# Leaving one token of each batch out of a projection, and one column out of each score tile

## The chip, the cores and the metric

One core of a Trainium2 chip. The metric is the device time of one execution of the whole program, in microseconds (us). A run is compared only with runs of the kernel before on the same chip.

## The reference, cut to what matters

128 batches of 64 tokens with 768 features go through two layers of attention on a graph. Everything is FP32.

```python
h = relu(layernorm(x))
for l in range(2):
    m_left  = einsum('bsh,oh->bso', h, W_left[l])
    m_right = einsum('bsh,oh->bso', h, W_right[l])
    u_left  = einsum('bih,bjh->bij', h, m_left)  / sqrt(768)
    u_right = einsum('bih,bjh->bij', h, m_right) / sqrt(768)
    # on and above the diagonal the left score counts, below it the right one
    u = u_left * triu(adj, k=0) + u_right * swapaxes(triu(adj, k=1), 1, 2)
    e = exp(u) * adj
    attention = e / (sum(e, axis=2) + 1e-10)
    h = relu(layer_norm(attention @ (h @ W_lin[l].T + b_lin[l])))
out = x + h
```

A right score is used only for j < i. So `m_right` of the last token of a batch (j = 63) is used by no row at all. That is what the change removes.

## The kernel before

Each layer has two passes over 16 blocks of 512 tokens (8 batches). Pass one makes `m_left` and `m_right` of a block ("project") and then, one block late, the scores and the softmax. Pass two makes the linear part, the attention times it, and the normalization. A projection is done as 15 products of sums of weight blocks and sums of token blocks, 256 tokens wide, whose results VectorE and ScalarE read out of the bank and add into `M`. The two halves k = 0 (left) and k = 1 (right) lie side by side in `M`, 64 columns each.

```python
# project(u, k): 15 products, each with 2 x 2 matmuls of 128 x 128 by 128 x 256
p = bank[at].rearrange("p (g t) -> p g t", g=2)
for g in range(2):
    for c in range(K2):
        nc.tensor.matmul(p[:, g], w[ORDER[i][0]][:, c, g * P:(g + 1) * P], b()[t][:, c, :],
                         start=(new and g == c == 0), stop=(c == K2 - 1), skip_group_check=True)
...
read(p.rearrange("p g (b s) -> p g b s", s=S),
     lambda o: M[u][:, o // 2 * K2:(o // 2 + 1) * K2, o % 2 * 4:o % 2 * 4 + 4, k, :], i, seen)
...
# scores(u): rows 0-31 of a batch need left 0-63 and right 0-30,
# rows 32-63 need left 32-63 and right 0-62
for e in (0, 32):
    nc.tensor.matmul(p[h * S + e:h * S + e + 32, q, e:e + 96],
                     ht[:, c, b * S + e:b * S + e + 32], mb[:, e:e + 96],
                     start=(c == 0), stop=(c == C - 1))
```

Of the kernel before, what the change touches and what calls it, by code (L numbers as in the profile page):

```python
# [13 lines left out]
ALU = mybir.AluOpType  # L14
# [3 lines left out]
def kernel(  # L18
# [24 lines left out]
    nc = tc.nc  # L43
    B, S, H = x.shape
    L = w_lin.shape[0]
    P = 128
    C = H // P
    HH = H // 2
    K2 = 2
# [5 lines left out]
    NB = B * S // T  # L55
# [13 lines left out]
    NBB = T // S  # L69
# [17 lines left out]
    def run(slot):  # L87
        if slot in plan:
            for f in plan.pop(slot):
                f()  # L90
        elif idle:
            f = idle.popleft()
            if f is not None:
                f()
# [14 lines left out]
    ORDER = ((8, "X", "ta", "+2"), (5, "Z", "u1", "-0+2"), (0, "X", "u2", "+3"), (1, "Y", "u3", "-3"),  # L109
             (12, "X", "B3", "-5"), (6, "V", "B0", "-2"), (2, "X", "td", "-4"), (4, "Y", "tb", "+1"),  # L110
             (10, "X", "B4", "+0-2"), (7, "V", "B1", "+3"), (3, "X", "u0", "+1-3"), (11, "Y", "te", "+0"),
             (13, "V", "tc", "-1"), (9, "Z", "tg", "+4"), (14, "V", "tf", "+5"))
# [31 lines left out]
    def added(eng, o, sign, a, b):  # L144
        (eng.tensor_add if sign == "+" else eng.tensor_sub)(o, a, b)  # L145
# [13 lines left out]
    def tokens_of(key):  # L159
        ht = HT[key]  # L160
        r = {f"B{2 * j + t}": ht[:, j * K2:(j + 1) * K2, t * TH:(t + 1) * TH] for j in range(3) for t in range(2)}
        r.update(TS.get(key, {}))
        return r

    def sums_t(key, eng=nc.gpsimd):
        ts = TS[key] = {}

        def one(o, s, m, n):
            t = big.tile([P, K2, TH], F32, name="ts", bufs=13)
            b = tokens_of(key)  # L170
            added(eng, t, s, b[m], b[n])
            ts[o] = t

        return [lambda x=x: one(*x) for x in T_SUMS]
# [8 lines left out]
    def read(p, to, i, seen):  # L183

        what = ORDER[i][3]
        for n in range(0, len(what), 2):
            sign, o = what[n], int(what[n + 1])
            if o not in seen:
                seen.add(o)
                nc.scalar.activation(to(o), p, AF.Copy, scale=1.0 if sign == "+" else -1.0)  # L190
            else:
                added(nc.vector, to(o), sign, to(o), p)
# [20 lines left out]
    for h in range(PAIR):  # L213
        r = slice(h * S, (h + 1) * S)
# [153 lines left out]
    def pass_one(l, aside):  # L368
        with tc.tile_pool(name=f"one{l}", bufs=2, reuse_waits="tile") as sp:
            ADJ, CHAIN, M = {}, {}, {}  # L370
# [25 lines left out]
            def project(u, k, just):  # L396


                b, w = lambda: tokens_of((1, l, u)), W[l, "lr"[k]]
                bank, seen = {}, set()  # L400
                for i, (at, t, _) in ((i, (o[1], o[2], o[3])) for i, o in enumerate(ORDER)):
                    new = i in FIRST
                    if new:
                        bank[at] = ps_st.tile([P, 2 * TH], F32, name=at)
                    p = bank[at].rearrange("p (g t) -> p g t", g=2)
                    for g in range(2):
                        for c in range(K2):
                            nc.tensor.matmul(p[:, g], w[ORDER[i][0]][:, c, g * P:(g + 1) * P], b()[t][:, c, :],  # L408
                                             start=(new and g == c == 0), stop=(c == K2 - 1), skip_group_check=True)
                        if g == 0:  # L410
                            run(30 * k + 2 * i)
                    if i == 0 and k == 0:
                        if u:
                            scores(u - 1)
                        M[u] = sp.tile([P, C, NBB, 2, S], F32, name="m", bufs=1)
                    read(p.rearrange("p g (b s) -> p g b s", s=S),
                         lambda o: M[u][:, o // 2 * K2:(o // 2 + 1) * K2, o % 2 * 4:o % 2 * 4 + 4, k, :], i, seen)
                    for f in just.get(i, ()):
                        f()
                    run(30 * k + 2 * i + 1)  # L420

            def scores(u):



                ht, m, adj = HT[1, l, u], M[u], ADJ[u]
                p = ps_aux.tile([P, 2, T], F32, name="aux")[:, 0].rearrange("p (q m) -> p q m", q=Q)
                for q in range(Q):
                    for c in range(C):
                        for h in range(PAIR):  # L430
                            b = q * PAIR + h
                            mb = m[:, c, b].rearrange("p k j -> p (k j)")
                            for e in (0, 32):
                                nc.tensor.matmul(p[h * S + e:h * S + e + 32, q, e:e + 96],  # L434
                                                 ht[:, c, b * S + e:b * S + e + 32], mb[:, e:e + 96],
                                                 start=(c == 0), stop=(c == C - 1))

                def chain():

                    wm = sp.tile([P, Q, 2, S], F32, name="wm", bufs=1)  # L440
                    for k in range(2):
                        nc.gpsimd.tensor_tensor(wm[:, :, k], adj[:, :, 1 - k],
                                                tri[:, k].unsqueeze(1).to_broadcast([P, Q, S]), op=ALU.mult)
                    yield
                    flat = wm.rearrange("p q k j -> p (q k j)")
                    for i in range(0, P, 32):
                        r = wm.rearrange("p q k j -> p q (k j)")[i:i + 32, :, i % S:i % S + 96]
                        nc.vector.tensor_tensor(r, p[i:i + 32, :, i % S:i % S + 96], r, op=ALU.mult)  # L448
                        if i % S:
                            yield  # L450
                    v = adj[:, :, 0, :]
                    nc.vector.tensor_add(v, wm[:, :, 0], wm[:, :, 1])
                    yield
                    nc.scalar.activation(v, v, AF.Exp, scale=ISTEMPER)
                    yield
                    nc.vector.tensor_mul(v, v, adj[:, :, 1, :])
                    s = stat.tile([P, Q], F32, name="s", bufs=2)
                    nc.vector.reduce_sum(s, v, axis=mybir.AxisListType.X)
                    yield
                    nc.vector.tensor_scalar_add(s, s, EPS_ATT)  # L460
                    nc.vector.reciprocal(s, s)
                    nc.vector.tensor_tensor(v, v, s.unsqueeze(2).to_broadcast([P, Q, S]), op=ALU.mult)
                    yield

                    at = flat[:, :Q * S].rearrange("p (g q i) -> p g q i", g=2, q=Q)
                    nc.vector.transpose(at.rearrange("p g q i -> p q g i"),
                                        v.rearrange("p q (g j) -> p q g j", g=2))
                    to = ATT[l][u].rearrange("(b g j) q (h i) -> b h g j q i", b=2, g=2, h=2)
                    for a in range(4):
                        for g in range(2):  # L470
                            nc.sync.dma_start(to[a // 2, a % 2, g], at[a * 32:(a + 1) * 32, g])

                CHAIN[u] = chain()

            just = {}
            if l == 0:
# [22 lines left out]
                t, w = deque(sums_t((1, 0, 0), nc.vector)), deque([vs[4], vs[3]] + vs[5:])  # L499
# [16 lines left out]
            for u in range(NB):  # L516
                slot = 0
                if u == 0:
                    if l == 0:
                        rs = sums_w(0, "r", nc.gpsimd)  # L520
                        put(16, lambda: hold(M[0][:, 0, 4, 0, :1]))
                        for n in range(0, len(rs), 3):
                            put(17 + n // 3, *rs[n:n + 3])
                    slot = 14 if l else 15
                if u + 1 < NB:
                    slot = put_all(slot, prepare(u + 1))
                    nxt = (1, l, u + 1)
                else:
                    put(8, lambda: load_h(2, l, 0))
                    slot = put_all(9, softmax(u - 1) + none * 4 + affine(2, l, 0))  # L530
                    nxt = (2, l, 0)
                assert slot <= 47
                put_sums_t(nxt, max(slot, 40), 2 if slot <= 40 else 1, 30)
                if u in aside:
                    aside[u]()
                for k in range(2):
                    project(u, k, just if k == 0 and u == 0 else {})
                assert not plan
# [298 lines left out]
```

## Time and profile before

| | before |
|---|---|
| time, median of the first measurement | 2777.05 us (4 runs, 2776.29 to 2777.66) |
| TensorE busy | 2744.7 us of a span of 2775.4 |
| matmul records | 18712 in all; 3840 of the right projection, 6144 of the scores |
| spacing of records with 256 columns | 215.8 ns |
| burst of 192 score records | 4.10 us |

The prediction shows the lines that this table rests on. A record is one matmul entry of the trace. All spacings in this document are distances between the recorded starts of two records, because the ends of matmuls are modelled and neighbours overlap.

### The profile page before, as it was taken

How to read it: one execution, taken by the hardware profiler on the slowest of the kernel's cores; microseconds unless marked ns; L12 is line 12 of the kernel's file. 1: busy time of each engine (PE TensorE's matmuls, PEld its weight loads, DVE VectorE, ACT ScalarE, POOL GpSimd, SP SyncE). 2: the span in 40 equal slices, each digit the busy share in tenths (PEclk: the TensorE clock that was granted, in tenths of full speed). 3: DMA queues.
4: the chain of work that ended last, by engine and by line, in shares of the span. 5: the costliest groups of instructions: out<-in, count | busy, mean ns of one | idle time of the engine just before them, and what ended most of it. 6: DMA issues, size and time to landing. Idle time of an engine off the chain costs nothing.

```text
span 2775.4 us, 46099 instructions
## 1 busy us (share of the span) xinstructions
PE 2744.7 (99%) x18712; PEld 2338.2 (84%) x18712; DVE 1338.8 (48%) x2208; ACT 843.6 (30%) x1469; POOL 1198.0 (43%) x940
## 2 busy tenths in 40 slices
PE   8999999999999999999999999999999999999998
PEld 6888888888888888888788888888888888888886
DVE  6455445545454332322345444543444334666667
ACT  3232223222221344444421211222122214544443
POOL 4332352224223456555432344223222335887886
PEclk9999999999999999999999999999999999999999
DMA  6523432343222243343555422343234204555555
GB/s 197 131 75 97 120 81 75 84 120 94 75 74 77 84 146 107 121 140 107 150 135 139 109 77 75 98 121 79 75 88 118 69 25 142 157 177 163 167 167 143
DMA packets 234068, 310.80 MB, mean 112 GB/s; under 512 B 54144, under 2 KB 184448, under 8 KB 225664
## 3 DMA queue, kind: packets, MB, share of 16 engines
q1 hardware_dynamic: 233696, 307.45, 40.2%
q8 instruction: 149, 2.44, 0.4%
q14 instruction: 63, 0.52, 0.1%
q10 hardware_dynamic: 160, 0.39, 0.0%
HBM read 202.91 MB, written 104.86 MB: 111 GB/s over the span
## 4 chain that ended last, share of the span: by engine, by line
PE 97%; DVE 2%; ACT 1%; DMA 0%; issue 0%; SPq 0%; DVEq 0%; ACTq 0%
PE X L408 24%; PE V L408 16%; PE X L737 12%; PE Y L408 12%; PE Z L408 8%; PE V L737 8%; PE Y L737 6%; PE aux L434 5%; PE Z L737 4%; PE aux L621 3%; DMA w_l<-in_w_left_dram 0%; DVE ts L145 0%; DVE wm L448 0%; DVE m L145 0%; DVE w_l L145 0%
## 5 line engine op out<-in xcount | busy, mean ns | idle before, releaser
L145 POOL TENSOR_TENSOR ts<-ht 128x512 f32<-128x512 f32 x441 | 586.0, 1340 | 1229.7 <-DMA ht<-h 422.8
L190 ACT ACTIVATE m<-X 128x512 f32<-128x512 f32 x256 | 152.4, 595 | 1114.5 <-PE X L408 591.3
L145 POOL TENSOR_TENSOR ts<-ht,ts 128x512 f32<-128x512 f32 x189 | 249.2, 1326 | 155.1 <-PE X L737 77.2
L145 DVE TENSOR_TENSOR m<-m,V 128x512 f32<-128x512 f32 x256 | 174.2, 681 | 270.4 <-PE V L408 270.3
L145 DVE TENSOR_TENSOR m<-m,X 128x512 f32<-128x512 f32 x256 | 163.8, 681 | 251.9 <-PE X L408 251.2
L737 PE MATMUL X<-w_n,ts 128*128 128x256 f32 x1024 | 244.1, 380 | 1.8 <-DVE hl L145 1.0
L408 PE MATMUL X<-ts,w_l 128*128 128x256 f32 x1024 | 242.8, 380 | 2.3 <-POOL w_l L145 1.7
L408 PE MATMUL X<-ts,w_r 128*128 128x256 f32 x1024 | 241.9, 379 | 0.0
L145 DVE TENSOR_TENSOR m<-m,Z 128x512 f32<-128x512 f32 x128 | 88.0, 687 | 312.1 <-ACT m L190 253.0
L408 PEld LDWEIGHTS X<-ts,w_l 128*128 128x128 f32 x1024 | 192.0, 190 | 32.9 <-DVE m L145 2.7
L737 PEld LDWEIGHTS X<-w_n,ts 128*128 128x128 f32 x1024 | 191.7, 190 | 33.1 <-DVE hl L145 2.8
L408 PEld LDWEIGHTS X<-ts,w_r 128*128 128x128 f32 x1024 | 192.3, 190 | 28.7
L258 ACT ACTIVATE ht<-ht,b_col,a_col 128x512 f32<-128x512 f32 x192 | 143.5, 804 | 130.4 <-DMA ht<-h 130.4
L737 PE MATMUL Y<-w_n,ts 128*128 128x256 f32 x768 | 182.5, 379 | 0.0
L408 PE MATMUL Y<-ts,w_l 128*128 128x256 f32 x768 | 181.4, 379 | 0.0
L408 PE MATMUL Y<-ts,w_r 128*128 128x256 f32 x768 | 181.4, 379 | 0.0
L190 ACT ACTIVATE hl<-X 128x512 f32<-128x512 f32 (+1 forms) x136 | 77.7, 571 | 330.3 <-PE X L737 327.2
L737 PEld LDWEIGHTS Y<-w_n,ts 128*128 128x128 f32 x768 | 145.8, 190 | 20.4 <-issue 0.6
L408 PEld LDWEIGHTS Y<-ts,w_r 128*128 128x128 f32 x768 | 145.9, 190 | 19.8
L408 PEld LDWEIGHTS Y<-ts,w_l 128*128 128x128 f32 x768 | 145.9, 190 | 19.9
L145 DVE TENSOR_TENSOR hl<-hl,X 128x512 f32<-128x512 f32 (+1 forms) x136 | 83.1, 652 | 146.5 <-PE X L737 135.5
L145 DVE TENSOR_TENSOR hl<-hl,V 128x512 f32<-128x512 f32 (+1 forms) x136 | 89.0, 655 | 127.8 <-PE V L737 127.3
(138 smaller groups left out, 4716.4 us busy)
## 6 DMA issues: line engine op xcount, KB each, us to landing
ht<-h SPq DMA_DIRECT2D x63, 1536.0 KB, 7.1
h<-xb SPq DMA_DIRECT2D x124, 384.0 KB, 6.0
z<-z SPq DMA_DIRECT2D x128, 192.0 KB, 2.9
x<-z SPq DMA_DIRECT2D x128, 192.0 KB, 8.3
x<-in_x_dram SPq DMA_DIRECT2D x120, 192.0 KB, 8.4
xr<-in_x_dram SPq DMA_DIRECT2D x120, 192.0 KB, 3.6
out_dram<-xr SPq DMA_DIRECT2D x120, 192.0 KB, 2.6
adj<-in_adj_dram SPq DMA_DIRECT2D x64, 128.0 KB, 2.7
```

The source lines that it names most:

```text
L145: (eng.tensor_add if sign == "+" else eng.tensor_sub)(o, a, b)
L190: nc.scalar.activation(to(o), p, AF.Copy, scale=1.0 if sign == "+" else -1.0)
L258: nc.scalar.activation(ht, ht, AF.Relu, bias=cols[1][:, c:c + 1], scale=cols[0][:, c:c + 1])
L408: nc.tensor.matmul(p[:, g], w[ORDER[i][0]][:, c, g * P:(g + 1) * P], b()[t][:, c, :], start=(new and g == c == 0), stop=(c == K2 - 1), ski ...
L434: nc.tensor.matmul(p[h * S + e:h * S + e + 32, q, e:e + 96], ht[:, c, b * S + e:b * S + e + 32], mb[:, e:e + 96], start=(c == 0), stop=(c ...
L621: nc.tensor.matmul(cx[k][i, m, :HH], at[j, q, :], hl[j, q, m * HH:(m + 1) * HH], start=True, stop=True)
L737: nc.tensor.matmul(p[:, n], b[t][:, c, r * P:(r + 1) * P], w[s][:, c, :], start=(i in FIRST and i not in PRELOAD and n == c == 0), stop=(c ...
```

## The change

The intent is to stream fewer columns through TensorE, which is busy for 99% of the span. The right projection leaves out the last token of each batch: 4 x 63 = 252 columns instead of 256. The score tiles lose the one column that nobody reads: 95 instead of 96. The last block of a pass keeps its 256.

```diff
+                ns = S - 1 if k and u < NB - 1 else S
+                bs = "p (b s) -> p b s"
...
-                    p = bank[at].rearrange("p (g t) -> p g t", g=2)
+                    p = bank[at][:, :NBB * ns].rearrange("p (g b s) -> p g b s", g=2, s=ns)
...
-                            nc.tensor.matmul(p[:, g], w[ORDER[i][0]][:, c, g * P:(g + 1) * P], b()[t][:, c, :],
+                            nc.tensor.matmul(p[:, g], w[ORDER[i][0]][:, c, g * P:(g + 1) * P],
+                                             b()[t][:, c, :].rearrange(bs, s=S)[:, :, :ns],
...
-                    read(p.rearrange("p g (b s) -> p g b s", s=S),
-                         lambda o: M[u][:, o // 2 * K2:(o // 2 + 1) * K2, o % 2 * 4:o % 2 * 4 + 4, k, :], i, seen)
+                    read(p, lambda o: M[u][:, o // 2 * K2:(o // 2 + 1) * K2, o % 2 * 4:o % 2 * 4 + 4, k, :ns],
+                         i, seen)
...
-                                nc.tensor.matmul(p[h * S + e:h * S + e + 32, q, e:e + 96],
-                                                 ht[:, c, b * S + e:b * S + e + 32], mb[:, e:e + 96],
+                                nc.tensor.matmul(p[h * S + e:h * S + e + 32, q, e:e + 95],
+                                                 ht[:, c, b * S + e:b * S + e + 32], mb[:, e:e + 95],
...
-                        r = wm.rearrange("p q k j -> p q (k j)")[i:i + 32, :, i % S:i % S + 96]
-                        nc.vector.tensor_tensor(r, p[i:i + 32, :, i % S:i % S + 96], r, op=ALU.mult)
+                        r = wm.rearrange("p q k j -> p q (k j)")[i:i + 32, :, i % S:i % S + 95]
+                        nc.vector.tensor_tensor(r, p[i:i + 32, :, i % S:i % S + 95], r, op=ALU.mult)
```

## The prediction

> **What bounds the kernel now.** I read the page from the top: busy shares, slices, chain, groups. Then I asked for the chain in order of time inside one block, for TensorE's waits, and for busy time in two windows.
>
> The busy shares and the chain that ended last:
>
> ```profile
> PE 2744.7 (99%) x18712; PEld 2338.2 (84%) x18712; DVE 1338.8 (48%) x2208; ACT 843.6 (30%) x1469; POOL 1198.0 (43%) x940
> ...
> PE 97%; DVE 2%; ACT 1%; DMA 0%; issue 0%; SPq 0%; DVEq 0%; ACTq 0%
> PE X L408 24%; PE V L408 16%; PE X L737 12%; PE Y L408 12%; PE Z L408 8%; PE V L737 8%; PE Y L737 6%; PE aux L434 5%; PE Z L737 4%; PE aux L621 3%; DMA w_l<-in_w_left_dram 0%; DVE ts L145 0%; DVE wm L448 0%; DVE m L145 0%; DVE w_l L145 0%
> ```
>
> TensorE is busy all the way, and the path that sets the end runs through it alone. A busy TensorE need not be at its peak, so the second question is whether its records follow each other at the streaming rate. The chain in order of time, within one block of pass one (columns: start, length, what):
>
> ```profile
> 468.74 4.10 PE aux L434 x192
> 472.83 1.92 PE Z L408 x8
> 474.76 1.73 PE X L408 x8
> 476.48 1.73 PE Y L408 x8
> 478.21 1.73 PE X L408 x8
> ...
> 493.75 1.73 PE Z L408 x8
> 495.48 1.73 PE V L408 x8
> 497.20 1.73 PE X L408 x8
> ```
>
> The reader should see an even beat. From 474.76 to 495.48 there are twelve groups of eight records: 20.72 / 96 = 215.8 ns a record, with no gap for a wait. L408 is the projection (left, then right), L434 the scores: 192 records in 4.10 us, 21.4 ns each, or 85.4 ns for four.
>
> The waits of TensorE, longest in total first:
>
> ```profile
> PE aux L333 <- ACT x L283: 8.7, 2, 7.8
> PE aux L434 <- issue: 1.7, 6, 0.4
> PE Z L408 <- issue: 1.7, 1, 1.7
> PE X L408 <- POOL w_l L145: 1.7, 1, 1.7
> ```
>
> Half of all waiting is the first transpose, before any projection. The right projection and the scores, as groups:
>
> ```profile
> L408 PE MATMUL X<-ts,w_r 128*128 128x256 f32 x1024 | 241.9, 379 | 0.0
> L408 PEld LDWEIGHTS X<-ts,w_r 128*128 128x128 f32 x1024 | 192.3, 190 | 28.7
> L434 PE MATMUL aux<-m,ht 128*32 128x96 f32 x6144 | 136.9, 247 | 1.8 <-issue 1.7
> ```
>
> The right projection never waits. A record lasts 379 ns but the next starts after 215.8 ns: durations overlap, so I cost with spacing, not with duration. The weight load takes 190 ns and has 28 ns idle before it: it fits inside the spacing with room. The count is twice the number of matmuls in the code (32 blocks x 15 products x 4 = 1920 for the right half; the six groups of w_r hold 1024 + 768 + 4 x 512 = 3840), so each matmul here runs as two records.
>
> **What the Trainium skill says.** "TensorE: Matmul & The Clock Gate", section Back-to-back issue gap, gives N / 2.4 + 2.5 ns for a warm array. With N = 512 that is 215.8 ns, which is what the chain shows for a record of 256 columns; with N = 192 it is 82.5 ns, against the 85.4 measured for four score records (the latter includes the ends of the burst). So a record costs two array cycles a column. "FP8 and Floating Point Precision", section TensorE Precision Notes, says that true FP32 takes four passes: two records of two cycles a column agree with it. "TensorEngine Tiling (Array Packing)", section Key Properties, says that tiles work independently; 21.4 ns a score record, a quarter of what one alone would need, agrees. "Advanced Engine Details and Errata", section Memory Cachelines, warns that lines are 16 bytes in SBUF and 8 bytes (two FP32 values) in PSUM, and that a non-contiguous pattern slows matmuls. The trace of before cannot test that: all its moving operands are contiguous rows.
>
> **The change part by part.** *Right projection.* Each moving operand shrinks from 256 contiguous columns to four runs of 63 with a step of 64, so 252, in all blocks of a pass but the last: 15 of 16 blocks, two layers, 120 records a block: 2 x 15 x 120 = 3600 records. Per record four columns go, each two cycles at 2.4 GHz: 8 / 2.4 = 3.33 ns (an estimate from the skill's gap formula). The trace gives a second estimate of the slope: (215.8 - 85.4) / (256 - 96) = 0.815 ns a column, 3.26 ns for four. Sum: 3600 x 3.33 = 12.0 us (11.7 with the slope of the trace). All of it is on the path, since the path goes through every one of these records and nothing else in those stretches. A right half should go from 120 x 215.8 = 25.9 us to 25.5 us, and a block from about 56.1 to 55.7 us.
>
> *Scores.* 6144 records of 96 columns become 95. Four go side by side, so there are 1536 steps, each one column shorter: 1536 x 0.833 = 1.3 us. This holds in all 32 blocks. I count it in full, though an odd number of columns may round up to 96.
>
> *Evictions.* VectorE and ScalarE read 504 elements for 512 in the right half, and 4x95 for 4x96 in the masked scores. At 681 ns for 512 elements an eviction can shrink by some 8 ns. VectorE is 48% busy and ScalarE 30%, and TensorE waits for neither in the right half, so this is worth nothing on the path. The place in the bank changes too: the second half now starts at element 252, an even one, so pairs of values stay aligned, and the output rows are adjacent, thus contiguous.
>
> *What stays.* Instruction counts and their order on every engine: the listing of both kernels shows the same rows with other shapes. No weight, transfer, semaphore wait or buffer is added or taken away. The left projection (3840 records), the linear pass (3840), the contexts and the two last blocks keep their size.
>
> Sum: 12.0 + 1.3 = 13.3 us, 0.48% of 2777.3: **2764.0 us**.
>
> **The rivals.**
> *A. The matmul does not gain from broken rows.* If reading costs a line or a pair at a time, a run of 63 costs as much as 64 (16 lines of four either way; 31 pairs and one half). Then the right projection gains nothing, the scores perhaps nothing either, and the time stays at 2776 to 2777. For it: the cacheline section, and 63 and 95 being odd. Against it: the spacing of before is exactly two cycles a column, that is limited by the array and not by the read, and the runs still start on 256-byte steps.
> *B. Each break between rows costs something.* Three breaks a record; a few cycles each, say 4, would be 3 x 4 / 2.4 = 5 ns, more than the 3.3 gained: 3600 x (5.0 - 3.3) = 6 us slower, less the scores: about 2782. For it: nothing in this trace, as no moving operand has two levels. To reach 2% slower (55.5 us) a record must lose 15.4 ns net, some 15 cycles a break after making good the gain; I hold that unlikely.
> *C. TensorE goes faster and meets another engine.* The right half would run 0.4 us ahead of GpSimd's sums of tokens, which the next left half needs, and of the evictions. Busy time in two windows of pass one:
>
> ```profile
> 300.00:950.00 650.00, 648.64 (x5048) 569.07 (x5040) 318.33 (x592) 153.94 (x226) 195.32 (x169) 1.00 0.33 87
> 1450.00:2290.00 840.00, 839.18 (x6351) 736.21 (x6340) 365.63 (x601) 174.53 (x286) 258.68 (x221) 1.00 0.34 89
> ```
>
> GpSimd (the fifth figure) is busy 30% of the time there, VectorE (the third) under 50%, the DMA engines a third. Against 0.4 us a block there is slack of tens of us. C would take back 1 to 2 us at most, at the first block, where GpSimd's weight sums are just in time, and where the left half, which is unchanged, does the waiting.
> *D. The weight load becomes the bound.* 190 ns long, against a new spacing of 212.5 ns: 22 ns remain, so no.
>
> **Range and chances.** I give the sum two chances in three. A, in full or in part, gets about one in five and puts the time between 2765 and 2777; B about one in eight, from 2778 up. The counted gain is exact work at an exact rate, so it can hardly be exceeded: under 2762 would need something that I do not see. Range 2762 to 2777, leaning upward from the estimate because all risks lie on that side. Faster by over 2% would need four times what the change removes: 0.5%. Slower by over 2% is B at its worst: 2.5%. Within 2%: 97%.
>
> **What would show it right or wrong.** In the profile after, the chain in order of time should show the groups of eight in a right half at 1.70 us (8 x 212.5 ns) and those of a left half still at 1.73; the burst of 192 scores at about 4.06 us; the records of w_r, in the form 128x252, at some 376 ns (379 less 3.3), with no idle time before them; TensorE's waits unchanged, with their 8.7 us for the first transpose. If the right half keeps 1.73, A is true; if it is above, B. If the groups shrink but the span does not, C: then a new wait stands in TensorE's list. The scores are judged alone: 4.10 us kept means that 95 columns cost what 96 do. The step I trust least is that a column left out of a broken row is a column less in time.

## The result, and the profile after

The changed kernel took 2765.01 us (median of 4 runs, 2761.76 to 2766.81), the kernel before 2777.05 us on the same chip. The ratio is 0.9955, with a 95% interval of 0.9938 to 0.9973. A ratio here is the mean time of one kernel's fast runs over the mean of the other's of the same rounds, so it is not quite the ratio of the medians. The result is correct.

The busy shares of the changed kernel, then its chain of work in order of time in a block of pass one (start, length, what):

```profile
PE 2734.1 (99%) x18712; PEld 2338.2 (85%) x18712; DVE 1336.8 (48%) x2208; ACT 842.3 (30%) x1469; POOL 1197.5 (43%) x940
```

```profile
472.00 1.73 PE X L412 x8
...
491.00 1.73 PE Z L412 x8
492.72 1.73 PE V L412 x8
494.45 1.70 PE X L412 x8
496.15 1.70 PE Z L412 x8
...
518.25 1.70 PE V L412 x8
519.95 1.73 PE X L412 x8
```

L412 is L408 of before, and L439 is L434. The border between the halves is plain: up to 494.45 the left half in groups of 1.73 us, from there the right half in groups of 1.70 us, and at 519.95 the next block's left half. In single starts, the 252-column records lie 212.50 ns apart, those with 256 columns 215.83 ns. The chain also has whole bursts of scores, here the first:

```profile
71.69 4.06 PE aux L439 x192
```

It was 4.10 us before. The groups (partitions x columns, type, count, busy time, mean duration, idle time before them):

```profile
L412 PE MATMUL X<-ts,w_r 128*128 128x252 f32 x960 | 223.6, 376 | 0.0
L412 PE MATMUL X<-ts,w_r 128*128 128x256 f32 x64 | 15.1, 379 | 0.0
L439 PE MATMUL aux<-m,ht 128*32 128x95 f32 x6144 | 135.9, 246 | 1.9 <-issue 1.5
```

Sixty-four records of this group kept their 256 columns: the last blocks. Nothing waits ahead of the right half. TensorE's waits, in total, times and longest:

```profile
PE aux L333 <- ACT x L283: 7.9, 2, 7.7
PE Z L412 <- issue: 1.9, 1, 1.9
PE aux L439 <- issue: 1.5, 5, 0.4
```

The list is that of before, with the first transpose on top. The accounts close as well. The span went from 2775.4 to 2763.4 us, so 12.0 us. The records say: 12.0 us less of streaming in the right half (3600 x 3.33 ns) and 1.0 us less in the scores with the waits inside their bursts, against 1.5 us more from seven records of the left half that ran at half speed. The rest is waits of some tenths. Those seven records follow a wait of TensorE that both kernels have. The timeline of TensorE in the changed kernel, and the windows around it (span, busy time of PE, PEld, DVE, ACT, POOL, then the granted clock):

```profile
78.69 1.59 PE L412 MATMUL Z<-ts,w_l 128*128 128x256 f32 x4 [1.88 <-issue]
```

```profile
76.00:79.00 3.00, 1.12 (x6) 0.85 (x5) 0.00 (x0) 0.46 (x1) 3.00 (x3) 1.00 1.09 377
79.00:83.00 4.00, 4.00 (x13) 3.21 (x12) 2.02 (x5) 0.60 (x1) 3.21 (x4) 0.57 0.15 53
83.00:90.00 7.00, 7.00 (x34) 6.17 (x33) 2.52 (x7) 3.32 (x5) 0.00 (x0) 1.00 0.00 0
```

After a wait of 1.9 us the mean granted clock of the 4 us from 79.00 was 0.57. In the profile of before the same place has a wait of 1.7 us and a clock of 1.00 after it, and in a second profile of the changed kernel (below) a wait of 1.8 us without such a stretch. So it belongs to this one execution and not to the change. It cost 1.5 us, more than the whole gain of the scores.

### The profile page after: what moved, and what is told of

The parts are those of the page before. It is cut to its first block, busy times and chain, and to the rows that moved or that the text cites. A ratio compares the mean times of both kernels' runs of the same rounds, so it can differ in the third digit from the quotient of the medians.

```text
span 2763.4 us, 46099 instructions
## 1 busy us (share of the span) xinstructions
PE 2734.1 (99%) x18712; PEld 2338.2 (85%) x18712; DVE 1336.8 (48%) x2208; ACT 842.3 (30%) x1469; POOL 1197.5 (43%) x940
## 4 chain that ended last, share of the span: by engine, by line
PE 97%; DVE 2%; ACT 1%; issue 0%; DMA 0%; SPq 0%; DVEq 0%; ACTq 0%
PE X L412 24%; PE V L412 16%; PE X L742 12%; PE Y L412 12%; PE Z L412 8%; PE V L742 8%; PE Y L742 6%; PE aux L439 5%; PE Z L742 4%; PE aux L626 3%; DVE ts L145 0%; DVE wm L453 0%; DVE m L145 0%; DVE w_l L145 0%; DMA x<-in_x_dram 0%
## 5 line engine op out<-in xcount | busy, mean ns | idle before, releaser
L190 ACT ACTIVATE m<-X 128x512 f32<-128x512 f32 (+1 forms) x256 | 151.5, 592 | 1102.8 <-PE X L412 586.0
L145 DVE TENSOR_TENSOR m<-m,V 128x512 f32<-128x512 f32 (+1 forms) x256 | 173.3, 677 | 267.0 <-PE V L412 266.9
L145 DVE TENSOR_TENSOR m<-m,X 128x512 f32<-128x512 f32 (+1 forms) x256 | 162.9, 677 | 248.1 <-PE X L412 247.4
L412 PE MATMUL X<-ts,w_l 128*128 128x256 f32 x1024 | 243.9, 381 | 1.7 <-POOL w_l L145 1.1
L412 PE MATMUL X<-ts,w_r 128*128 128x252 f32 (+1 forms) x1024 | 238.7, 376 | 0.0
L145 DVE TENSOR_TENSOR m<-m,Z 128x512 f32<-128x512 f32 (+1 forms) x128 | 87.5, 683 | 309.7 <-ACT m L190 251.4
L412 PEld LDWEIGHTS X<-ts,w_l 128*128 128x128 f32 x1024 | 193.0, 191 | 32.6 <-DVE m L145 2.7
L412 PEld LDWEIGHTS X<-ts,w_r 128*128 128x128 f32 x1024 | 192.0, 190 | 26.0
L412 PE MATMUL Y<-ts,w_l 128*128 128x256 f32 x768 | 181.4, 379 | 0.0
L412 PE MATMUL Y<-ts,w_r 128*128 128x252 f32 (+1 forms) x768 | 179.1, 376 | 0.0
L412 PEld LDWEIGHTS Y<-ts,w_l 128*128 128x128 f32 x768 | 145.9, 190 | 19.9
L412 PEld LDWEIGHTS Y<-ts,w_r 128*128 128x128 f32 x768 | 145.9, 190 | 17.4
```

Of the source, the lines that this page charges most:

```text
L145: (eng.tensor_add if sign == "+" else eng.tensor_sub)(o, a, b)
L190: nc.scalar.activation(to(o), p, AF.Copy, scale=1.0 if sign == "+" else -1.0)
```

## The experiments

**Theory:** TensorE is bound by columns streamed; each takes two cycles, wherever it lies in its row. **Rivals:** broken rows cost something or eat the gain (A and B of the prediction); faster streaming meets another engine (C); weight loads become the bound (D). Eleven kernels ran. The first five below were timed in five rounds on one chip, with medians of 2776.35 to 2776.40 us for the kernel before; the others had one run each, so their state is unknown. The runs of one value and the two with a broken bank were on another chip, where one run of the kernel before took 2777.98 us.

**The changed kernel once more.** No edit.

> The changed kernel once more, as the yardstick of this call. Theory (columns streamed set the time): 12.0 us from the right projection and 1.3 us from the scores, so about 13.3 us under the kernel before, ratio 0.9952. The first measurement gave 12.0 us with a spread of 5 us between runs; if the scores give nothing (an odd width is rounded up) it should settle near 12.0, ratio 0.9957.

Measured: 2763.24 us (2762.75 to 2768.93), ratio 0.9958 (0.9945 to 0.9970). Four of five runs lie within 1.1 us; the fifth is 5.7 us above the median, and it is the one with the profile. TensorE's waits there have a line that is 0.5 us in the first profile:

```profile
PE X L412 <- ACT m L190: 3.8, 2, 3.3
```

The cause stands in ScalarE's timeline, in the first block of the second layer, and in the windows of all engines around it:

```profile
1420.91 0.59 ACT L190 ACTIVATE m<-X 128x504 f32<-128x504 f32 x1 [2.81 <-PE X L412]
1427.21 1.52 ACT L258 ACTIVATE ht<-ht,b_col,a_col 128x512 f32<-128x512 f32 x2 [5.71 <-DMA ht<-h]
1428.63 0.57 ACT L190 ACTIVATE m<-X 128x504 f32<-128x504 f32 x1
```

```profile
1424.00:1430.00 6.00, 2.72 (x14) 2.10 (x13) 0.00 (x0) 2.79 (x5) 0.00 (x0) 1.00 0.74 171
1430.00:1434.00 4.00, 4.00 (x12) 3.27 (x11) 1.27 (x2) 2.49 (x4) 3.24 (x3) 0.57 0.71 212
```

ScalarE sat for 5.71 us before scaling a block of tokens that a load had not yet brought. The eviction that comes after it in this timeline started at 1428.63, and TensorE stood 3.3 us for it. Then the mean granted clock of 4 us was 0.57 and seven more records ran at half speed, 7 x 208 ns = 1.5 us. Together that is 4.8 of the 5.7 us. The load took 11.6 us in this run and 7.1 us in the profile of before. The profiled run of the contiguous variant below shows the same chain. So two of the five profiles with 252 columns have this stall, and none of the other eight. That is too few to tell whether the change makes it likelier: the kernel before had no run of over 2778.66 us in 15, but the kernel with the scores alone, which keeps the 256 columns, had one of 2781.36 us, without a profile.

**Projection alone.**

```diff
# against the changed kernel: scores with 96 columns where they can be read
- mb[:, e:e + 95]
+ mb[:, e:e + (95 if e else 96)]
# and the same width for the output and for the mask
```

> Right projection with 252 columns as in the change; scores with 96 columns for rows 0 to 31 of a batch and 95 for rows 32 to 63 (the last column is never written, so 96 can't be read there). Correct result. Theory: a step of four score tiles lasts as long as its widest, so 192 score records take 4.10 us as before, and the whole gains 12.0 us: ratio 0.9957. Rival (each score tile is paid for singly): 0.65 us of the scores' 1.3 is kept, 12.7 us.

Measured: 2763.89 us (2763.03 to 2765.34), ratio 0.9957. The right half keeps 212.50 ns. A burst of scores takes 4091 ns from its first start to the next instruction, where before has 4098, the changed kernel 4058, and payment tile by tile would give 4078. So a step of four tiles is nearly as long as its widest, and the projection makes nearly all of the gain: 2776.35 - 2763.89 = 12.5 us.

**Scores alone.**

```diff
- ns = S - 1 if k and u < NB - 1 else S
+ ns = S
```

> Projection with 256 contiguous columns as before, scores with 95. Correct result. Theory: 1536 steps of four tiles, 0.83 ns each: 1.3 us less, ratio 0.9995; records of the scores 81.7 ns per four for 82.5, a burst of 192 in 4.06 us for 4.10. Rival (odd width costs as much as 96): nothing, and the burst stays at 4.10 us.

Measured: 2774.94 us (2774.35 to 2781.36), ratio 1.0001 (0.9989 to 1.0014). The time can't tell: one run of 2781.36 outweighs everything, and the medians differ by 1.4 us. The trace can: a burst that ran without a wait (some 19 of the 32) took 4058 ns for 4098, that is 40 ns for 48 steps, 0.83 ns each. An odd width is not rounded up. The chain of this run:

```profile
71.96 4.06 PE aux L439 x192
```

**The last blocks too.**

```diff
- ns = S - 1 if k and u < NB - 1 else S
+ ns = S - 1 if k else S
```

> The change applied to the last block of a pass as well: 240 more records of 252 columns. Correct result. Theory: 240 x 3.33 ns = 0.8 us less than the changed kernel, 2764.2 us or ratio 0.9949 to the kernel before. Rival (at the end of a pass the scores wait for the last evictions anyway, so an earlier end of the projection only lengthens that wait): under 0.3 us. Either way too little to tell by the times alone; the records of the last blocks (212.5 ns apart) and TensorE's waits at the end of each pass tell it.

Measured: 2762.14 us (2761.58 to 2765.18), ratio 0.9953, correct. Its median is 1.1 us below that of the changed kernel in the same rounds, where 0.8 was expected, and all 3840 records stand 212.5 ns apart. It is the fastest kernel by its median, but the intervals overlap widely, so that it beats the changed one is not shown by the times. The traces speak for it: the two last right halves took 25.59 us each for 25.99, and the bursts of scores behind them 4.31 and 4.42 us for 4.44 and 4.53. The wait there did not grow, so the rival is out and the 0.8 us are kept.

**No breaks between rows.**

```diff
- b()[t][:, c, :].rearrange(bs, s=S)[:, :, :ns],
+ b()[t][:, c, :NBB // 2 * ns],
```

> The changed kernel with its right projection reading the first 252 tokens in one contiguous run instead of four runs of 63 (wrong result on purpose: other tokens land in the columns). Theory: breaks between rows cost nothing, spacing 212.5 ns and the time of the changed kernel, ratio 0.9952 to before. Rival (a break costs something, part of the gain of four columns is lost to it): faster than the changed kernel, by 1.25 ns x 3600 = 4.5 us for every cycle a break costs.

Measured: 2764.59 us (2761.90 to 2768.44), ratio 0.9956 (wrong result). The records with one run of 252 lie 212.5 ns apart like those with four runs of 63: the mean over all of them without the stall described above is the same to a tenth of a ns. Three breaks cost nothing, so rival B is out at the size of this change.

**Sixty-four runs of four.** In the kernel before, right half only:

```diff
- b()[t][:, c, :],
+ b()[t][:, c, :].rearrange("p (x y z) -> p y x z", x=2, z=4) if k else b()[t][:, c, :],
```

> The kernel before, right projection only, in all blocks: 256 columns read in 64 runs of 4 values (16 bytes) that jump 128 values to and fro (wrong result on purpose: the order of the columns). No column less, 63 breaks a record where the change has 3. Theory (breaks are free): spacing 215.8 ns, time of before, 2777 us. Rival (a break costs c cycles): 63 x c / 2.4 ns a record, 3840 records: 101 us more for each cycle.

Measured: 2776.11 us; spacing 215.83 ns. Sixty-three breaks a record cost nothing either.

**Runs of one value.** The same edit with z=1.

> As r8 with runs of one value: every moving value of the right projection lies 128 values (512 bytes) from the one before (wrong result on purpose: order of the columns). Theory (the array's two cycles a column hide the reading): 215.8 ns, 2776 us as r8. Rival[...]: up to twice the streaming time, 3840 x 213 ns = 819 us more.

Measured: 2994.95 us. Here the reading shows. The chain in the right half of a block, with groups of eight that took 1.73 us:

```profile
488.69 2.19 PE Z L408 x8
490.88 2.19 PE X L408 x8
493.06 2.19 PE Y L408 x8
```

The spacing is 273.2 ns, 57.4 ns more than 215.8; times 3840 that is 220 us, and the time rose by 217. So a broken row can cost, as rival A feared, but not with runs of four; with jumps from value to value it takes 27% more, not 100%. Runs of two and three values were not tried, nor was another length of jump, so the mechanism stays open.

**The same order in the bank.** Both edits again, with the output written in the same broken order, so that the results are correct (the warning meant in the second expectation is the one that the prediction cites):

```diff
- nc.tensor.matmul(p[:, g], ...
+ nc.tensor.matmul(p[:, g].rearrange("p (x y z) -> p y x z", x=2, z=4) if k else p[:, g], ...
```

> As r8 (64 runs of 4), and the output is written to the bank in the same broken order, so the result is correct. Theory: 215.8 ns, 2776 us. Rival (a broken pattern in the bank slows the matmul[...]): some ns a record, 3.8 us for each ns.

Measured: 2775.98 us, 215.83 ns.

> As r9 with the output written in the same order, each value 512 bytes from the one before; correct result. If the cacheline warning of the skill holds for FP32 at two cycles a column, this is the run to show it: up to 819 us more. If columns alone count, 215.8 ns and 2776 us.

Measured: 2995.11 us, 273.2 ns. Both equal their partners above to the tenth of a ns. A broken output cost nothing beside a broken input. A broken output with a contiguous input was not run: with runs of one value a cost of the output of up to 57 ns could hide behind that of the input.

**Many fewer columns.** In the kernel before, right half only, the second of each two accumulating matmuls is narrowed:

```diff
+ n = 192 if k and c else TH
- nc.tensor.matmul(p[:, g], ..., b()[t][:, c, :],
+ nc.tensor.matmul(p[:, g, :n], ..., b()[t][:, c, :n],
```

> The kernel before, right projection only: of each pair of accumulating matmuls the second has 192 contiguous columns for 256 (wrong result on purpose). 1920 records lose 64 columns. Theory (columns streamed): spacing of those records 162.5 ns, 1920 x 53.3 = 102 us less, about 2675 us. Rival (the weight load, 190 ns long in the records, becomes the bound): spacing not under 190 ns, at most 50 us less, 2727 us or more. Rival (TensorE runs ahead into evictions or GpSimd's sums): spacing as in the theory but waits of TensorE that grow by as much as the span falls short.

Measured: 2690.51 us, 86 us less. (It passed the comparison although it leaves work out; that speaks of the tolerance.) The narrow records are 162.5 ns apart, as the theory says. Of the 16 us that are missing from 102, 12.4 lie between the starts of records in the right halves, nearly all of it where a product begins in bank X. The list of TensorE's matmul waits does not show them. They stand in that of its weight loads (PEld), where before has 2.7 us for VectorE's evictions and no line for ScalarE's:

```profile
PEld X L409 <- DVE m L145: 10.0, 46, 0.5
PEld X L409 <- ACT m L190: 5.8, 28, 0.4
```

The other 4 us are in the left halves, mostly records at half speed in the first two blocks. The chain shows the plain groups, 8 x (215.8 + 162.5) / 2 = 1.51 us, and at two places in each right half one that is longer, here the first:

```profile
322.90 1.51 PE Y L409 x8
324.42 1.66 PE X L409 x8
326.07 1.51 PE V L409 x8
```

The longer one begins a new product in bank X, whose eviction the two lines above name.

With n = 128:

> As the run before with 128 columns in the second matmul (wrong result on purpose). Theory: spacing 109.2 ns, 1920 x 106.7 = 205 us less, about 2572 us. Rival (weight load as bound): spacing not under 190 ns, 2727 us or more. Rival (another engine): GpSimd, VectorE or ScalarE named in new waits of TensorE.

Measured: 2620.14 us, 156 us less (wrong result). Two narrow records stand 109.1 ns apart while the weight load's record is 191 ns long on average (and 167.0 us of busy time for 1024 of them is 163 ns each, so these records overlap each other):

```profile
L409 PEld LDWEIGHTS X<-ts,w_r 128*128 128x128 f32 x1024 | 167.0, 191 | 25.3 <-DVE m L145 10.5
```

So its duration is no bound, and rival D is out for the change. A small rest stays open: two of each four spacings are 2.5 ns longer than the formula of the prediction gives, 4.8 us in all. Of 205 us, 49 were lost, and evictions appear in the waits of the matmuls too:

```profile
PE X L409 <- ACT m L190: 15.6, 29, 1.9
PE aux L333 <- ACT x L283: 7.8, 1, 7.8
PE X L409 <- POOL ts L145: 4.1, 1, 4.1
```

Rival C is real, then, for larger cuts: nothing at 4 columns off every record, 16% of the gain lost at 64 off every second one, 24% at 128 (single runs, with their chance events in them).

## Why the prediction was right or wrong

**The bound** (TensorE at its streaming rate): right. **Two cycles a column**: right to the hundredth of a ns; 215.83 - 212.50 = 3.33 ns for four columns, 53.3 for 64, 106.7 for 128. Its source, "TensorE: Matmul & The Clock Gate", section Back-to-back issue gap, gives 212.5, 162.5 and 109.2 ns for N = 504, 384 and 256; measured were 212.50, 162.5 and 109.1.

**The right projection, 12.0 us**: right; the projection alone gave 12.5 us by medians and 12.0 by its records. **The scores, 1.3 us**: right in the trace (40 ns x 32 = 1.28 us), not resolved by the time. The worry that 95 rounds up to 96 was unfounded. **Evictions worth nothing**: right, the waits ahead of the right half stayed at zero; the means of the groups that mix left and right fell by 4 ns (681 to 677 for V), and since only the right ones are shorter, that is 8 ns for each of these, as expected.

**The sum, 2764.0**: 2765.01 was measured, then 2763.24. By medians the change is worth 12.0 and 13.1 us, by the 95% intervals 8 to 17 and 8 to 15 us. What is short of 13.3 is within what single executions lose by chance to stalls and half-speed stretches. So that the medians came within 1 us of the forecast is partly luck; the sum is confirmed by the records, where 3600 x 3.33 ns and 32 x 40 ns were found.

**The rivals.** A and B were given a third of the chances together. Both are refuted for this change, and the experiments show how far off they were: a break every four values was still free. For A the prediction leaned on a sentence about non-contiguous patterns that stands, in the section it cites, under PSUM, the output, and not under the reading of an operand. What weakened the prediction was not a wrong step but that no matmul of the kernel before had a broken row, so the point that it trusted least could not be read from any view. C did not come at this size, but it was placed wrongly. The prediction looked for it at the first block, in GpSimd's weight sums, and in the left half, and counted tens of us of slack a block from the busy shares. With 64 columns off every second record a right half would be 3.2 us shorter, and waits for evictions already stood at bank X in every right half: a busy share does not tell when a buffer comes free. The wait that did appear in some executions of the changed kernel sits at the start of the second layer, where ScalarE waits for a load. That wait is not shown to come from the change. D fell as foreseen, with far more room than the 22 ns that the prediction counted: it took the load's record length for its cost, the same mistake that it had avoided for matmuls.

**Range and chances**: the result lies inside 2762 to 2777 and within 2%. The single run of 2761.76 lies just under it, so the lower edge was set tight.

## What to carry to other kernels

Where the chain shows matmuls at an even beat with no waits, count columns: two cycles each in FP32 here, and leaving out columns between others cost nothing here as long as four values or more stayed adjacent (63 and 4 were tried). Price such a change by the spacing of starts and check it there too, because the chance events of single executions (5.7 us in one here) are half as large as such a gain. A larger cut of the same kind should be checked against the evictions first, since they took back a sixth to a quarter of the gain in the wider trials.

## What the Trainium skill lacked or had wrong

- "Advanced Engine Details and Errata", section Memory Cachelines, says that any non-contiguous pattern in PSUM significantly slows matmuls. For FP32 matmuls here it was not seen: an output in runs of four values kept 215.83 ns, and one with each value 512 bytes from the one before had the same spacing as a contiguous one (273.2 ns with it and without it, the input being broken in both, so that a smaller cost could hide).
- The same section has no figure for a broken SBUF read. For FP32 moving operands: runs of 63 and of 4 values cost nothing, runs of 1 with jumps of 512 bytes cost 57.4 ns a record of 256 columns (27%).
- "TensorE: Matmul & The Clock Gate", section Back-to-back issue gap, calls N / 2.4 + 2.5 ns the isolated gap and says that real streams with weight loads have about 131 ns at N = 512. In this stream of load and matmul pairs the formula held exactly (215.83 ns for 512 cycles), once each FP32 matmul is counted as two records of two cycles a column; the page does not say how FP32 is split into records.
- The same page, section What's actually happening, puts the idle time after which the clock halves at about 3.4 us, in a free-running window. Here a wait of 1.9 us was followed by a mean granted clock of 0.57 over 4 us in one execution, and one of 1.7 us at the same place in another was not.
